# Attention sums of layer 0: where the halves of the weighted values are added, when GpSimd adds beta, and how many buffers hold the experts' results

## The chip, the cores and the metric

The kernel runs on one core of a Trainium2 chip. The metric is the device time of the launch in microseconds (us). The kernel before has a median of 5901.39 us over three runs (5897.41 to 5913.06). A difference of 0.3% is 17.7 us.

## The reference, cut to what matters

The program is two layers over 3125 nodes with 256 features and 100000 edges. Layer 0 adds a graph network and a mixing network to the nodes, then a routed feed-forward network with 16 experts. Layer 1 has other networks, which the change doesn't touch; a few loads for it begin early. The parts of layer 0 that are concerned:

```
def transformer_conv(x, edge_index, ...):            # runs twice, 4 heads of 64
    q, k, v = x @ wq + bq, x @ wk + bk, x @ wv + bv  # each reshaped to (n, heads, 64)
    src, dst = (edge_index[0], edge_index[1])
    qi, kj, vj = (q[dst], k[src], v[src])
    alpha = jnp.sum(qi * kj, axis=-1) / math.sqrt(out_ch)
    alpha = ...                                      # softmax over the edges of each dst
    out = jax.ops.segment_sum(vj * alpha[..., None], dst, num_segments=n)
    return out.reshape(n, heads * out_ch) + x @ ws + bs

xn = _layernorm(x)
x = x + gnn(xn) + mix(xn)                            # gnn: conv, batch norm, leaky relu, twice
x = x + ffn(_layernorm(x))

def ffn(x):                                          # 16 experts, the best 2 of each node
    topk_vals, topk_idx = top_k(x @ gate_w + gate_b, 2);  topk_w = softmax(topk_vals)
    moe = sum of topk_w * (relu(x @ w1[e] + b1[e]) @ w2[e] + b2[e]) over the 2 experts
    y = x + moe
    return (y - mean(y)) / sqrt(var(y) + EPS) * gamma + beta
```

## The kernel before

**The two convolutions** (`l0_gnn_slots`, L1318, with the class `SlotOrder`, L1063) put the nodes into 25 blocks of 128, sorted by degree. A block has a number of slots (`SLOTS`, L627; 833 in all): slot j holds one edge of each of the 128 nodes. A block's slots are cut into steps, 63 in a convolution, and a step has one or two buffers `kv` of 6 to 8 slots: 63 first buffers (b = 0 in the code) and 52 second buffers (b = 1). A step goes through these stages:

- GpSimd gathers key and value rows of the edges' sources, one indirect DMA for each slot (L635, called in `gathers`, L1085). The pool has four `kv` buffers, so a gather into one waits until the sums have read it.
- VectorE multiplies keys by queries (L1114) and reduces them (L1117), adds a bias and finds the maximum (L1127 to L1131); ScalarE takes the exponential (L1141).
- `values` (L1143): VectorE sums the weights (L1147), multiplies the values by them (L1153), and then adds the second half of the buffer's slots to the first half (L1158, the **half-add**): of m slots, m // 2 sums of pairs remain, and a slot left over where m is odd.
- `sums` (L1160): TensorE multiplies each remaining slot by the identity and accumulates in PSUM (tile `cps`, L1168), so that all slots of the step are summed. The profile shows two matmul instructions for each of these calls[...].
- ScalarE copies the sum out (`result`, L1175), and a block's steps are joined.

The order on TensorE, VectorE and ScalarE is written by hand (`manual_schedule`, L1364): the list `PATTERN` (L1060) names the stages of neighbouring steps in turn ("V0" and "V1" are `values` for first and second buffers, "P0" and "P1b" their sums), and at each "m" a piece of the mixing network (`l0_mix_pieces`, L1500) is put in, so many by planned cost (`Filling`, L838; `mix`, L1363). GpSimd's and SyncE's order is set by a scheduler.

**The routed network** (`l0_ffn_routed`, L2034). SyncE first fills the table `xs` in HBM with zeros (L2059, 16 DMAs of 512 KB). For each of 7 groups of up to four tiles of 125 nodes, VectorE and TensorE find the two best experts and each node's slot number there (`sloti`, L2132). GpSimd scatters the nodes' rows into `xs`, two indirect DMAs for each tile, 50 in all (L2135, kept in the list `sent`). After the loop GpSimd adds beta to `xcur`, the nodes' running sum, seven additions of up to 125x1024 elements (L2148); the scheduler has put these among the groups' work, ahead of the first scatter. Expert 0's load (L2158) waits for all 50 scatters. The experts follow on TensorE (L2166, L2174, L2182). Then for each tile two gathers (L635, tile `g`, from pool `f_back`) bring an expert's rows back, and VectorE adds them (L2196), normalises, and adds `xcur` (L2206). After that come loads and tables of layer 1, whose edge rows (`ea`) GpSimd gathers too. A reduction over partitions (L3302), written at the end of the program, is run by GpSimd after the last scatter.

Of the kernel before, what the change touches and what calls it, by code (L numbers as in the profile page):

```python
# [14 lines left out]
ALU = mybir.AluOpType  # L15
# [4 lines left out]
P = 125  # L20
D = 256
# [269 lines left out]
def after(k, ins, others):  # L291

    for other in others:
        k.tc.add_manual_dep(
            ins.ins, other.ins.name,
            mybir.DependencyInfo(mybir.DependencyClass.Sync, mybir.DependencyReason.DATA),
            reason="rows of the table",
        )
# [295 lines left out]
def l0_gnn(k, x, conv, y_mix, xcur):  # L594
# [32 lines left out]
SLOTS = [  # L627
    64, 43, 41, 39, 38, 37, 36, 35, 35, 34, 33, 33, 32, 32, 31, 30, 30, 29, 29, 28, 27, 26, 25, 24, 22
]
# [282 lines left out]
def steps(ns):  # L912

    n = -(-ns // SUB)
    subs = [ns // n + (i < ns % n) for i in range(n)]
    return [subs[i : i + 2] for i in range(0, n, 2)]
# [146 lines left out]
class SlotOrder:  # L1063
# [78 lines left out]

    def values(self, n, b):  # L1143

        nc, t, H = self.k.nc, self.steps[n], self.HEADS
        if b == 0:
            nc.vector.tensor_reduce(  # L1147
                self.tile(t["i"])["den"][:, t["c"]], t["w"].rearrange("p s h -> p h s"), axis=AX.X,
                op=ALU.add,
            )  # L1150
        m, kv, b0 = t["subs"][b], t["kv"][b], sum(t["subs"][:b])
        v = self.heads(kv[:, :m, D:])
        nc.vector.tensor_tensor(  # L1153
            v, v, t["w"][:, b0 : b0 + m].unsqueeze(3).to_broadcast([128, m, H, D // H]), op=ALU.mult
        )
        half = m // 2
        v = kv[:, :half, D:]
        nc.vector.tensor_tensor(v, v, kv[:, half : 2 * half, D:], op=ALU.add)  # L1158

    def sums(self, n, b):  # L1160

        t = self.steps[n]
        m, kv, b0 = t["subs"][b], t["kv"][b], sum(t["subs"][:b])
        if b == 0:
            t["acc"] = self.pp.tile([128, 512], F32, name="cps", tag="cps")
        left = [*range(m // 2), *range(m // 2 * 2, m)]
        for j in left:
            self.k.nc.tensor.matmul(  # L1168
                t["acc"][:, :D], self.k.ident, kv[:, j, D:], start=(b0 + j == 0),
                stop=(b == len(t["subs"]) - 1 and j == left[-1]),  # L1170
            )
# [146 lines left out]
def l0_gnn_slots(k, dram, order, a, y, pp, pq, cw, filling, tmp):  # L1318
# [4 lines left out]
    nc, N = k.nc, k.N  # L1323
    NQ = len(SLOTS)
# [35 lines left out]
    bmv = cw.tile([128, 2, 2], F32, name="bmv")  # L1360
    sc = cw.tile([128, 2], F32, name="sc")
    sh = cw.tile([128, 2], F32, name="sh")
    mix = filling(2 * 3 * sum(len(steps(n)) for n in SLOTS) + NQ)  # L1363
    with k.tc.manual_schedule(engines=ORDERED):  # L1364
        mix.ahead(30.0)
        prev = None
        for n in (1, 2):
            if n == 2:
                weights = l0_qs_weights(k, cw, a, 2)
            wq, bq, wsk, bs, gam, bet = weights  # L1370
# [85 lines left out]
            with ExitStack() as st:  # L1456
# [4 lines left out]
                sent, ps = [], None  # L1461
# [451 lines left out]
def layer0(k, dram, x, order_of, a, y):  # L1913
# [3 lines left out]
    with ExitStack() as st:  # L1917
        wts, one, mwp, hp, hp2, cw, pp, cp, pq = pools(
            k, st,
            [("m_w", 1), ("m_one", 1), ("m_work", 1), ("m_hid", 1), ("m_hT", 2), ("c_w", 1)],  # L1920
            [("m_ps", 4), ("c_ps", 2), ("c_qa", 2)],
        )
        for g0, ng in k.groups:
            nc.sync.dma_start(y[:, g0 : g0 + ng], tok(x)[:, g0 : g0 + ng])
        tmp = ExitStack()
        order = order_of(pools(k, tmp, [("n_one", 1), ("n_wk", 4)]), cp)
        with ExitStack() as s2:
            (wp,) = pools(k, s2, [("m_ln", 1)])
            mv, rs = ln_stats(k, wp, y)
            for i in range(NT):  # L1930
                ln_tile(k, y[:, i], y[:, i], mv, rs, i)
        pieces = l0_mix_pieces(k, dram, sub("L0_mix_"), y, wts, one, mwp, hp, hp2, pp)
        gout, sent = l0_gnn_slots(
            k, dram, order, sub("L0_gnn_"), y, cp, pq, cw, lambda n: Filling(pieces, n), tmp
        )
        (wp,) = pools(k, st, [("c_add", 2)])
        for g0, ng in k.groups:
            xt = wp.tile([P, 4, D], F32, name="xt", tag="xt")
            part = wp.tile([P, 4, D], F32, name="part", tag="part")
            nc.sync.dma_start(xt[:, :ng], tok(x)[:, g0 : g0 + ng])  # L1940
            after(k, nc.sync.dma_start(part[:, :ng], tok(gout[0:k.N, :])[:, g0 : g0 + ng]), sent)
            nc.gpsimd.tensor_tensor(xt[:, :ng], xt[:, :ng], part[:, :ng], op=ALU.add)
            nc.vector.tensor_tensor(y[:, g0 : g0 + ng], y[:, g0 : g0 + ng], xt[:, :ng], op=ALU.add)
# [90 lines left out]
def l0_ffn_routed(k, dram, xcur, a, over, a1):  # L2034
# [4 lines left out]
    nc, N, NT = k.nc, k.N, k.NT  # L2039
# [9 lines left out]
    with ExitStack() as st:  # L2049
        big, one, wts, wp, gp, bp, hp, pp = pools(  # L2050
            k, st,
            [("f_big", 1), ("f_one", 1), ("f_w", 3), ("f_wk", 3), ("f_g", 2), ("f_back", 8), ("f_hid", 2)],
            [("f_ps", 2)],
        )
        zero = big.tile([128, 4 * D], F32, name="zero")
# [9 lines left out]
        bet = one.tile([P, D], F32, name="bet")  # L2065
# [23 lines left out]
        sent = []  # L2089
        for g0, ng in k.groups:  # L2090
# [7 lines left out]
            for j in range(ng):  # L2098
                at = ps[:P, j * NE : j * NE + NE]
                for c in range(2):  # L2100
                    m = nc.tensor.matmul(
                        at, xT[:, c, j * P : j * P + P], gw[:, c, :], start=(c == 0), stop=False
                    )
# [29 lines left out]
            for i in range(g0, g0 + ng):  # L2133
                for r in range(2):
                    ins = nc.gpsimd.indirect_dma_start(  # L2135
                        out=xs, in_=acc[:, i], in_offset=None,
                        out_offset=bass.IndirectOffsetOnAxis(ap=sloti[:, r, i : i + 1], axis=0),
                    )
# [6 lines left out]
        nc.vector.tensor_reduce(over[:P, 0:1], full, axis=AX.X, op=ALU.max)  # L2145
        for g0, ng in k.groups:
            x = xcur[:, g0 : g0 + ng]
            nc.gpsimd.tensor_tensor(x, x, bet.unsqueeze(1).to_broadcast([P, ng, D]), op=ALU.add)  # L2148

        b1 = one.tile([128, NE, 4], F32, name="b1")  # L2150
        nc.sync.dma_start(b1, a["b1"].rearrange("e (c p) -> p e c", p=128))
# [1116 lines left out]
def fast(k, dram, a, out, over, dump):  # L3268

    sub = lambda pre: {s[len(pre) :]: v for s, v in a.items() if s.startswith(pre)}  # L3270

    def show(name, xcur):
        if dump is not None and name in dump:
            k.nc.sync.dma_start(tok(dump[name]), xcur)

    with ExitStack() as st:
        (keep,) = pools(k, st, [("order", 1)])
        order_of = lambda tmp, pp: node_order(
            k, dram, a["src"], a["dst"], keep, tmp, pp, over[:, 0:2]
        )  # L3280
        with ExitStack() as s2:
            (xpool,) = pools(k, s2, [("xcur", 1)])
            xcur = xpool.tile([P, k.NT, D], F32, name="xcur")
            order = layer0(k, dram, a["x"], order_of, a, xcur)
            show("x1", xcur)
            tabs = l0_ffn_routed(k, dram, xcur, sub("L0_ffn_"), over[:, 2:3], sub("L1_gnn_"))
            show("x2", xcur)
        layer1(k, dram, a, out, tabs, order, show)
# [56 lines left out]
```

## Time and profile before

The profiled execution took 6377.69 us with a span of 6375.9 us and a mean TensorE clock of 0.832 of full speed. It is 8% longer than the median without a profile.

| stretch of the profiled span, us | work |
|---|---|
| 0 to 322 | order of the nodes, tables |
| 322 to 1655 | convolution 1, pieces of the mixing network beside it |
| 1655 to 1790 | between the convolutions |
| 1790 to 3116 | convolution 2, pieces of the mixing network beside it |
| 3116 to 3225 | batch norm, rows |
| 3225 to 3356 | choice of experts, scatters |
| 3356 to 3602 | 16 experts |
| 3602 to 3770 | results gathered, first tables of layer 1 |
| 3770 to 6376 | layer 1 |

| line | engine, operation | count | busy us | mean ns |
|---|---|---|---|---|
| L1153 | VectorE, values by weights | 230 | 477.3 | 2075 |
| L1158 | VectorE, half-add | 230 | 241.9 | 1052 |
| L1168 | TensorE, sums | 1792 | 520.1 | 439 |
| L635 | GpSimd, gathers `kv` (both layers) | 2499 | 2459.2 | 984 |
| L635 | GpSimd, gathers `g` | 50 | 63.4 | 1269 |

The views name engines PE (TensorE matmul), PEld (TensorE weight load), DVE (VectorE), ACT (ScalarE), POOL (GpSimd), and SP (SyncE); a q behind the name is the engine's queue that issues DMAs. "x8" counts instructions. In brackets stands the idle time before an instruction and what ended it; "issue" means that nothing the profile shows was waited for. PEclk is the granted share of TensorE's full clock.

### The profile page before, as it was taken

The page shows a single profiled execution, that of the slowest core. Times are in us where ns is not written, and L with a number is a line of the kernel's source. Part 1 is how long each engine was busy: PE and PEld are TensorE (multiplying, and loading weights), DVE is VectorE, ACT ScalarE, POOL GpSimd, SP SyncE. Part 2 cuts the span into 40 slices and gives each one's busy share as a digit, 9 for nine tenths or more (in the row PEclk, how much of TensorE's full clock was granted, in tenths as well). Part 3 has the DMA queues.
Part 4 walks back from the last instruction along what each step waited for, and adds up shares of the span by engine and source line. Part 5 has one row for each costly group of instructions (what it writes and reads, how often), then busy time and mean ns, then how long its engine had stood idle before and what let it go on. Part 6 is the DMA issues. An engine that isn't in the chain of part 4 may idle for free. (4 is left out here: it accounts for less than half of the span.)

```text
span 6375.9 us, 48523 instructions
## 1 busy us (share of the span) xinstructions
PE 4695.9 (74%) x15769; PEld 2692.1 (42%) x15769; DVE 4360.7 (68%) x6216; ACT 1584.1 (25%) x3284; POOL 2934.7 (46%) x2945
## 2 busy tenths in 40 slices
PE   3367887678856887678749756787888777786768
PEld 2144554455534555456436423333333333333335
DVE  5287888888578787988531345667777666777657
ACT  1032333222323323332311101222222222221222
POOL 2465665666365665666450233334344333434321
PEclk8687998889977898888859877888897888888879
DMA  4366665666365665666444353334344333434320
GB/s 139 92 179 179 184 188 158 183 180 179 128 188 169 180 179 170 181 186 188 134 143 145 120 174 115 110 105 142 111 122 135 116 112 115 130 108 132 112 69 21
DMA packets 374280, 908.49 MB, mean 142 GB/s; under 512 B 94268, under 2 KB 170074, under 8 KB 373892
## 3 DMA queue, kind: packets, MB, share of 16 engines
q0 software_dynamic: 232624, 725.48, 39.1%
q1 hardware_dynamic: 137412, 168.23, 8.2%
q10 hardware_dynamic: 3982, 11.59, 0.5%
q8 instruction: 128, 2.10, 0.1%
q14 instruction: 134, 1.10, 0.1%
HBM read 813.62 MB, written 91.30 MB: 142 GB/s over the span
## 5 line engine op out<-in xcount | busy, mean ns | idle before, releaser
L635 POOL DMA_INDIRECT kv<-kvtab,slots x2499 | 2459.2, 984 | 2111.7 <-PE acc L1023 872.9
L2599 DVE TENSOR_TENSOR kv<-kv,e 128x1024 f32<-128x1024 f32 (+1 forms) x448 | 504.2, 1138 | 404.6 <-PE e L2594 173.6
L2594 PE MATMUL e<-weT,eaT 128*128 128x512 f32 (+1 forms) x896 | 555.7, 718 | 164.8 <-ACT eaT L2593 79.7
L1168 PE MATMUL cps<-kv,ident 128*128 128x256 f32 x1792 | 520.1, 439 | 145.4 <-issue 90.1
L1114 DVE TENSOR_TENSOR kv<-kv,qa 128x1792 f32<-128x1792 f32 (+2 forms) x230 | 478.6, 2081 | 87.9 <-DMA kv<-kvtab,slots 74.9
L1168 PEld LDWEIGHTS cps<-kv,ident 128*128 128x128 f32 x1792 | 386.4, 222 | 291.1 <-issue 159.0
L1117 DVE TENSOR_REDUCE al<-kv 128x28 f32<-128x1792 f32 (+2 forms) x230 | 479.4, 2085 | 7.9
L1153 DVE TENSOR_TENSOR kv<-kv,qa 128x1792 f32<-128x1792 f32 (+2 forms) x230 | 477.3, 2075 | 0.0
L1873 PE MATMUL mm<-w,hid 128*125 128x256 f32 x1600 | 406.0, 400 | 67.8 <-issue 33.8
L1855 PE MATMUL mm<-hTm,w 128*128 128x500 f32 (+1 forms) x896 | 384.8, 573 | 71.3 <-issue 24.2
L1873 PEld LDWEIGHTS mm<-w,hid 128*125 128x125 f32 x1600 | 307.9, 198 | 148.3 <-issue 66.6
L2594 PEld LDWEIGHTS e<-weT,eaT 128*128 128x128 f32 (+1 forms) x896 | 163.4, 220 | 404.2 <-issue 235.6
L1023 PE MATMUL acc<-kv,ident 128*128 128x256 f32 x896 | 252.0, 442 | 63.7 <-DVE kv L1020 58.9
L1855 PEld LDWEIGHTS mm<-hTm,w 128*128 128x128 f32 x896 | 168.4, 204 | 230.5 <-issue 165.4
L1023 PEld LDWEIGHTS acc<-kv,ident 128*128 128x128 f32 x896 | 196.4, 224 | 141.8 <-DVE kv L1020 89.9
L1545 PE MATMUL mm<-ident,xh 125*128 125x125 f32 x400 | 105.8, 359 | 194.5 <-ACT xh L1535 111.7
L2593 ACT COPY eaT<-e 128x128 f32<-128x128 f32 (+1 forms) x448 | 110.1, 267 | 555.6 <-PE e L2591 297.3
L1158 DVE TENSOR_TENSOR kv<-kv 128x768 f32<-128x768 f32 (+1 forms) x230 | 241.9, 1052 | 7.9
L985 DVE TENSOR_TENSOR kv<-kv,qa 128x1792 f32<-128x1792 f32 (+2 forms) x115 | 238.9, 2077 | 6.4 <-issue 5.2
L989 DVE TENSOR_REDUCE al<-kv 128x56 f32<-128x1792 f32 (+2 forms) x115 | 238.7, 2076 | 4.6 <-issue 3.6
L1014 DVE TENSOR_TENSOR kv<-kv,al 128x1792 f32<-128x1792 f32 (+2 forms) x115 | 235.0, 2080 | 0.0
L140 PE MATMUL mm<-wqv,hTm 128*125 128x512 f32 x400 | 196.5, 630 | 9.4 <-issue 3.9
(414 smaller groups left out, 7873.0 us busy)
## 6 DMA issues: line engine op xcount, KB each, us to landing
kv<-kvtab,slots POOLq DMA_INDIRECT x2499
w<-in_L_ffn_w_dram SPq DMA_DIRECT2D x32, 512.0 KB
qd<-qT SPq DMA_DIRECT2D x24, 500.0 KB
kvtab<-st SPq DMA_DIRECT2D x12, 1000.0 KB
qT<-qd SPq DMA_DIRECT2D x24, 500.0 KB
xTg<-xcols SPq DMA_DIRECT2D x24, 500.0 KB
w<-in_L_mix_W_dram SPq DMA_DIRECT2D x8, 1024.0 KB
xs<-zero SPq DMA_DIRECT2D x16, 512.0 KB
```

The source lines that it names most:

```text
L635: return k.nc.gpsimd.indirect_dma_start(out=out, out_offset=None, in_=table, in_offset=bass.IndirectOffsetOnAxis(ap=index, axis=0),)
L985: nc.vector.tensor_tensor(kv[:, :m, :D], kv[:, :m, :D], q.unsqueeze(1).to_broadcast([128, m, D]), op=ALU.mult,)
L1023: nc.tensor.matmul(acc[:, :D], k.ident, kv[:, j, D:], start=(b0 + j == 0), stop=(kv is bufs[-1][2] and j == left[-1]),)
L1114: nc.vector.tensor_tensor(kv[:, :m, :D], kv[:, :m, :D], q.unsqueeze(1).to_broadcast([128, m, D]), op=ALU.mult)
L1117: nc.vector.tensor_reduce(t["al"][:, b0 : b0 + m], self.heads(kv[:, :m, :D]), axis=AX.X, op=ALU.add)
L1153: nc.vector.tensor_tensor(v, v, t["w"][:, b0 : b0 + m].unsqueeze(3).to_broadcast([128, m, H, D // H]), op=ALU.mult)
L1158: nc.vector.tensor_tensor(v, v, kv[:, half : 2 * half, D:], op=ALU.add)
L1168: self.k.nc.tensor.matmul(t["acc"][:, :D], self.k.ident, kv[:, j, D:], start=(b0 + j == 0), stop=(b == len(t["subs"]) - 1 and j == left[-1]),)
L1855: nc.tensor.matmul(ps[:, :w_], W["w1"][:, c, j * 128 : j * 128 + 128], o["hT"][:, c, :w_], start=(c == 0), stop=(c == 1),)
L1873: nc.tensor.matmul(ps[:P, :D], s["hid"][:, c, j * P : j * P + P], W["w2"][:, c, :], start=(c == 0), stop=False,)
L2594: nc.tensor.matmul(e[:, :n].rearrange("p b d -> p (b d)"), eaT[r], weT[r, :n].rearrange("p b d -> p (b d)"), start=True, stop=True,)
L2599: nc.vector.tensor_tensor(t, t, e[:, :n].unsqueeze(2).to_broadcast([128, n, 2, D]), op=ALU.add)
```

## The change

- The half-add (L1158) is done for second buffers alone. For first buffers, TensorE sums all m slots.
- The count of points over which the mixing network's pieces are spread is written `1 * NQ` in place of `NQ`, which is the same number.
- The pool `f_back`, in which the gathered results of the experts lie, has 14 buffers in place of 8.
- The seven additions of beta wait for the last scatter (`after` adds a dependency on `sent[-1:]`).

```diff
@@ values, L1142
-        half = m // 2
-        v = kv[:, :half, D:]
-        nc.vector.tensor_tensor(v, v, kv[:, half : 2 * half, D:], op=ALU.add)
+        if b == 1:
+            half = m // 2
+            v = kv[:, :half, D:]
+            nc.vector.tensor_tensor(v, v, kv[:, half : 2 * half, D:], op=ALU.add)
@@ sums, L1160
-        left = [*range(m // 2), *range(m // 2 * 2, m)]
+        left = [*range(m // 2), *range(m // 2 * 2, m)] if b == 1 else range(m)
@@ l0_gnn_slots, L1363
-    mix = filling(2 * 3 * sum(len(steps(n)) for n in SLOTS) + NQ)
+    mix = filling(2 * 3 * sum(len(steps(n)) for n in SLOTS) + 1 * NQ)
@@ l0_ffn_routed, L2052
-            [("f_big", 1), ("f_one", 1), ("f_w", 3), ("f_wk", 3), ("f_g", 2), ("f_back", 8), ("f_hid", 2)],
+            [("f_big", 1), ("f_one", 1), ("f_w", 3), ("f_wk", 3), ("f_g", 2), ("f_back", 14), ("f_hid", 2)],
@@ l0_ffn_routed, L2146
-            nc.gpsimd.tensor_tensor(x, x, bet.unsqueeze(1).to_broadcast([P, ng, D]), op=ALU.add)
+            ins = nc.gpsimd.tensor_tensor(
+                x, x, bet.unsqueeze(1).to_broadcast([P, ng, D]), op=ALU.add
+            )
+            after(k, ins, sent[-1:])
```

The two programs, built and set side by side engine by engine, differ as follows. VectorE lacks 126 half-adds, 78 of 128x768 and 48 of 128x1024 elements, and nothing else is moved there. TensorE has 426 further calls of L1168, that is 852 matmul instructions. ScalarE and SyncE have the same instructions in the same order. On GpSimd the seven additions come after the 50 scatters and after the reduction over partitions (L3302), with the instruction that loads their library now directly ahead of them; and of the 50 gathers of results, 26 in place of 16 come ahead of layer 1's first `ea` gather.

## The prediction

> **What bounds the kernel now.** I read first the busy times by stretch. They show time, busy us of each engine (with instructions), granted TensorE clock (PEclk), DMA share and GB/s for the two convolutions, the end of the choice of experts, and the experts:
>
> ```profile
> core 0: us, PE busy (x) PEld busy (x) DVE busy (x) ACT busy (x) POOL busy (x), PEclk, DMA share, GB/s
> 322.00:1640.00 1318.00, 1004.69 (x3700) 676.96 (x3700) 1090.44 (x1502) 392.28 (x794) 824.01 (x827) 0.86 0.61 178
> 1760.00:3110.00 1350.00, 1014.20 (x3729) 684.86 (x3730) 1119.12 (x1512) 414.70 (x847) 822.47 (x829) 0.85 0.61 178
> 3340.00:3540.00 200.00, 180.27 (x672) 120.66 (x673) 35.63 (x73) 33.00 (x48) 8.10 (x8) 0.95 0.44 141
> ```
>
> In the convolutions DVE is 83% busy and PE 75 to 76%: neither alone is the bound, and they hand work to each other in a written order. So the question is who waits for whom at the half-add. The second view is that line's own: duration (min/median/max) and waiters (us, times).
>
> ```profile
> L1158 DVE TENSOR_TENSOR kv<-kv x230: 957/959/1284, 321.1 to 3111.0; 128x768 f32<-128x768 f32 x75, 128x1024 f32<-128x1024 f32 x40
> who waited for it (us, times):
>   PEld cps L1168: 67.5, 31
>   PE cps L1168: 50.7, 30
> ```
>
> PE waits for half-adds about 60 times. The timeline shows one place (start, duration), DVE first and then PE:
>
> ```profile
> 599.03 2.28 DVE L1153 TENSOR_TENSOR kv<-kv,qa 128x2048 f32<-128x2048 f32 x1
> 601.34 1.23 DVE L1158 TENSOR_TENSOR kv<-kv 128x1024 f32<-128x1024 f32 x1
> ```
>
> ```profile
> 598.56 1.99 PE L1873 MATMUL mm<-w,hid 128*125 128x256 f32 x8
> 602.62 1.99 PE L1168 MATMUL cps<-kv,ident 128*128 128x256 f32 x8 [2.07 <-DVE kv L1158]
> 604.45 1.89 PE L1873 MATMUL mm<-w,hid 128*125 128x256 f32 x8
> ```
>
> The sums begin 0.05 us after the add's end (602.57), and PE was idle 2.07 us ahead of them. I compared each add's end with its sums' start so, row by row. Of 126 first buffers, PE waits for the add in 69 (start within 0.6 us of its end), and is idle ahead of these 133 us in all; in 57 it comes 1 to 13 us later. For second buffers it is never sooner than 3.4 us: their adds are covered, and they stay.
>
> Third, the dispatch. GpSimd's scatters and PE's wait stand in its timeline:
>
> ```profile
> 3229.37 17.61 SPq L2059 DMA_DIRECT2D xs<-zero  x16
> 3274.05 0.72 POOL L2148 TENSOR_TENSOR xcur<-xcur,bet 125x256 f32<-125x256 f32 x1 [1.00 <-DVE acc L103]
> 3275.16 1.21 POOL L2135 DMA_INDIRECT xs<-acc,sloti  x1 [0.39 <-issue]
> 3348.36 1.19 POOL L2135 DMA_INDIRECT xs<-acc,sloti  x1 [0.30 <-issue]
> 3355.92 1.97 PE L2166 MATMUL tp<-ident,xe 128*128 128x128 f32 x8 [42.62 <-DMA xe<-xs]
> ```
>
> All betas come before the first scatter; 50 scatters run without a gap; PE waits 42.62 us for what they bring.
>
> [...] a block of 8 sums takes 1.99 us warm and up to 3.78 us cold, and slices with PE busy 105 of 160 us have PEclk 0.79, with 133 of 160 0.93. [...] DVE's L1977, usually 0.2 us, took 2.12 us beside a beta, while L2119, with an operand in PSUM, kept 0.16. [...] the trace has 5.60 us of idle time before the reduction L3302.
>
> **Half-adds.** Removed: 78×0.96 + 48×1.22 ≈ 133 us of DVE (durations from the row and the timeline above). What lies on the path decides. I walked each convolution back from its end, at each instruction to its releaser or its predecessor on the engine, whichever ended later: of 1336 us, DVE has 716 and PE 410 in the first, 662 and 444 in the second. 78 of the 126 adds are on it, worth 51.0 + 33.0 = 84 us: −84.
>
> Added: 426 sums (3.38 for a first buffer). A warm block gives (1.99 − 0.38)/7 = 0.23 us an instruction, 0.455 us a sum, so 1.54 us a buffer; the line's mean is 520.1/896 = 0.58 us, since 32 of the 126 blocks are cold. All 426 would be 194 to 247 us. In 66 buffers the sums are on the path (in 31 with the add too): 220 extra sums, 100 us warm, 128 at the mean. I take 107, near warm, as 94 of 126 blocks are. Lower bound: half, 50, if the other path takes over; upper: 128.
>
> A third term: PE gets busier, from 76% to about 84% of a step. By the slices above (0.14 of clock for 28 us of 160, 17%) its clock rises by 0.07, and the 854 us of PE on the path shrink by 3 to 4%: −30; bounds 0 and −45. Together −84 + 107 − 30 = **−7**, bounds about −60 and +44. The terms almost cancel, and that is the case's difficulty. A fit of the 124 steps' times to their PE and DVE times (0.62 and 0.75 us each) gives +23 to +37 without the warmer clock, about zero with it.
>
> Three things hang on this. ScalarE's L1175 comes after the sums, 52.7 us of waits now. A first `kv` buffer comes free 0.5 us later (1.54 − 1.03) where PE waited for the add, and 1.54 where not: GpSimd's gathers already wait 287.7 us for the sums, but GpSimd is idle 38% there, so I price it at zero; DVE waits 42.3 us for gathers in convolution 2, which bounds what this can double to. The mixing pieces keep their places.
>
> **Count of points.** The same number: 0.
>
> **Betas.** Out of the way, the first scatter waits for its slot numbers (ready at 3256.1 in the trace) and the zeros. DMA share is 1.03 until 3260, 0.46 to 3265 and 0.00 after, so the zeros land at about 3262; [...] 3264 in place of 3275.2. Later groups' numbers are ready every 3.4 to 14.0 us (3268.8, 3282.8, 3293.5, 3303.8), a group of eight scatters takes 8×1.494 = 11.95, so GpSimd meets them (the third's at 3287.9, the fourth's at 3299.9, the fifth's at 3311.8). PE's wait falls by 11.2: **−11**; bounds −17 (zeros not binding) and 0.
>
> The seven betas (6×2.34 + 0.72 ≈ 15 us), with the library's load ahead of them, now lie beside the experts, where GpSimd is idle 246 us; L2206, which reads `xcur`, comes 270 us later. Nothing else is queued behind them on GpSimd until 3601.9; the reduction L3302 comes ahead. Experts' DVE work reads PSUM with at most one SBUF operand[...]. SP's and ACT's DMA issues don't move.
>
> **Fourteen buffers.** Gathers of results go every 1.51 us from 3606.8, with no stall until 3658.5; then they wait 6.9, 2.3 and 20.3 us for buffers, and the last goes at 3715.9. But VectorE last waits for such a gather at 3638 (4.23 us); later it waits for table writes (17.87 us at 3705), and GpSimd idles 51.67 us at the end. The waits removed are off the path: −1, bounds −4 and +3 (ten gathers pass ahead of `ea`, 15 us, whose DMAs meet the loads).
>
> **Sum.** −7 − 11 − 1 = −19 against the profiled 6377.7: 6359. I carry the difference in us to the median, where DVE times should be the same: 5901.4 − 19 = **5882 us**.
>
> **The rivals.**
> *VectorE's gain counts, PE has room.* For it: DVE is busier, and 133 us of idle PE ahead of the waiting sums holds 69×1.54 = 106. Against: that idle time is spread unevenly. With half of the sums' path time hidden (+50), −15 of clock: −49, and −12: 5840. Chance 0.2.
>
> *PE becomes the bound (slower).* Place: the 47 first buffers where the add, but not the sums, is on the path; their 163 extra sums cost 74 us warm. It decides where PE's idle time ahead of the sums, plus the add's 1.03, is under 1.54, that is from under 0.5 us of idle. If half come onto the path (+37) and the clock gives 15 in place of 30: −84 + 107 + 37 − 15 = +45, and −12: +33, 5934. For it: 57 sums that come late already. Against: DVE has the longer share of the path. Chance 0.3.
>
> *The convolutions net to nothing, and only the dispatch counts:* 5889. It lies inside the forecast. [...]
>
> **How the numbers follow.** Forecast 0.5 (convolutions −25 to +25: 5864 to 5914), VectorE 0.2 (5822 to 5864), PE 0.3 (5914 to 5950). A measurement can tell about 0.3%, 17.7 us. Faster by more (under 5883.7): half of the forecast and all of the VectorE case, 0.45. Slower (over 5919.1): 0.25, nearly all of the PE case. Between: 0.30. Cases of both signs hold the chance; the forecast's own range is 5864 to 5914. The whole range leaves out half of the VectorE case and a quarter of PE's: 5838 to 5942.
>
> **What would show it.** Convolution stretches: DVE busy down by 67 us each, PE up by 95 to 125, PEclk from 0.86 towards 0.92, the length within 25 us of before. Waits of PE for L1153 where it waited for L1158. First scatter near 3264 less the convolutions' shift, i.e. PE's wait for `xe` near 31 us. Experts still 246 us long. VectorE's waits after 3638 unchanged. I am wrong if PEclk stays (then +20), if the first scatter comes late, or if the sums' blocks become cold.

## The result, and the profile after

The kernel after takes 5832.99 us (four runs, 5827.11 to 5836.81) against 5899.9 us for the kernel before: ratio 0.9881, 95% interval 0.9863 to 0.9899, **67 us faster**. The prediction was 5882 us with a range from 5838 to 5942; the sign was right and the time lies below the range. The profile that the prediction was read from is of an execution of 6377.69 us, not 5900 (one chip here runs this kernel in some 6445 us and three others in some 5900), so times by stage below are taken from a second profile of the kernel before, of an execution of 5896.65 us, and from the profile after, whose execution took 5829.55 us. In the code after, the half-add is L1160, the values' multiplication L1154, the sums L1170, the scatters L2137, beta L2150.

| from the profiles at 5896.65 and 5829.55 us | before | after | difference |
|---|---|---|---|
| start to the end of convolution 2's sums | 2913.8 | 2864.1 | -49.6 |
| from there to the first zero fill | 110.3 | 110.7 | +0.4 |
| first zero fill to first scatter | 45.7 | 26.2 | -19.5 |
| first scatter to the experts' first transpose | 80.6 | 81.4 | +0.8 |
| experts and return, to layer 1's first `xg` gather | 409.7 | 410.8 | +1.1 |
| layer 1 | 2334.8 | 2334.4 | -0.4 |

The busy times by stretch in the kernel after (convolutions, and a stretch from the dispatch into the experts):

```profile
core 0: us, PE busy (x) PEld busy (x) DVE busy (x) ACT busy (x) POOL busy (x), PEclk, DMA share, GB/s
318.00:1532.00 1214.00, 1055.02 (x4232) 751.40 (x4231) 1043.20 (x1471) 401.13 (x810) 807.67 (x831) 0.91 0.67 194
1660.00:2864.00 1204.00, 1046.66 (x4168) 743.91 (x4168) 1039.99 (x1443) 417.49 (x848) 781.44 (x806) 0.91 0.66 195
3000.00:3300.00 300.00, 248.22 (x938) 173.90 (x939) 72.78 (x276) 47.76 (x75) 74.74 (x58) 0.85 0.41 133
```

PE and DVE are now equally busy in the convolutions, 86 to 87% each, and PE is no longer the one with room.

Of the half-adds that stay, the view of the line in the kernel after shows:

```profile
L1160 DVE TENSOR_TENSOR kv<-kv x104: 957/959/1235, 324.4 to 2844.8; 128x768 f32<-128x768 f32 x72, 128x1024 f32<-128x1024 f32 x32
...
who waited for it (us, times):
  PEld cps L1170: 0.5, 2
```

Next to nobody waits for second buffers' adds (0.5 us). PE's waits stand at the multiplication, in the view of that line:

```profile
L1154 DVE TENSOR_TENSOR kv<-kv,qa x230: 1720/2011/2281, 319.9 to 2854.1; 128x1792 f32<-128x1792 f32 x63, 128x2048 f32<-128x2048 f32 x40, 128x1536 f32<-128x1536 f32 x12
...
who waited for it (us, times):
  PEld cps L1170: 82.4, 37
  PE cps L1170: 63.1, 25
```

The dispatch, from the timeline of the kernel after:

```profile
2974.86 18.19 SPq L2061 DMA_DIRECT2D xs<-zero  x16
2999.67 0.15 DVE L2134 CAST sloti<-slot 125x8 int32<-125x8 f32 x1
3001.11 1.21 POOL L2137 DMA_INDIRECT xs<-acc,sloti  x1 [30.30 <-DMA b<-in_L_ffn_b_dram]
3074.99 1.19 POOL L2137 DMA_INDIRECT xs<-acc,sloti  x1 [0.30 <-issue]
3082.55 1.75 PE L2171 MATMUL tp<-ident,xe 128*128 128x128 f32 x7 [26.89 <-DMA xe<-xs]
3089.41 14.58 POOL L2150 TENSOR_TENSOR xcur<-xcur,bet 125x1024 f32<-125x1024 f32 x7 [7.17 <-issue]
```

In the second profile of before, the first scatter comes 45.7 us behind the first zero fill; here it is 26.2 us. The slot numbers end 1.3 us ahead of it (2999.82), but they are not what it follows: the semaphores, in the experiment on the betas, show that it follows the last zeros. The DMA named in its bracket is one that counts on a semaphore which the zeros use too. The betas run as one block beside expert 0.

### The profile page after: what moved, and what is told of

The parts are those of the page before. It is cut to its first block, busy times and chain, and to the rows that moved or that the text cites. A ratio compares the mean times of both kernels' runs of the same rounds, so it can differ in the third digit from the quotient of the medians.

```text
span 5827.8 us, 50130 instructions
## 1 busy us (share of the span) xinstructions
PE 4671.1 (80%) x16621; PEld 2785.9 (48%) x16621; DVE 4216.7 (72%) x6090; ACT 1582.9 (27%) x3284; POOL 2901.4 (50%) x2945
## 5 line engine op out<-in xcount | busy, mean ns | idle before, releaser
L635 POOL DMA_INDIRECT kv<-kvtab,slots x2499 | 2425.6, 971 | 1742.1 <-PE acc L1023 691.6
L1170 PE MATMUL cps<-kv,ident 128*128 128x256 f32 x2644 | 688.8, 415 | 64.4 <-DVE kv L1154 63.1
L1170 PEld LDWEIGHTS cps<-kv,ident 128*128 128x128 f32 x2644 | 548.9, 211 | 214.3 <-DVE kv L1154 82.4
L2599 PE MATMUL e<-weT,eaT 128*128 128x512 f32 (+1 forms) x896 | 516.6, 673 | 66.4 <-ACT eaT L2598 64.7
L1154 DVE TENSOR_TENSOR kv<-kv,qa 128x1792 f32<-128x1792 f32 (+2 forms) x230 | 475.3, 2074 | 0.0
L1857 PE MATMUL mm<-hTm,w 128*128 128x500 f32 (+1 forms) x896 | 364.4, 551 | 30.5 <-DVE xcur L1883 21.7
L1875 PE MATMUL mm<-w,hid 128*125 128x256 f32 x1600 | 378.5, 385 | 1.8 <-ACT hid L1865 1.8
L1023 PE MATMUL acc<-kv,ident 128*128 128x256 f32 x896 | 268.3, 463 | 76.9 <-DVE kv L1020 72.0
L1865 ACT ACTIVATE hid<-mm,b 128x500 f32<-128x500 f32 (+1 forms) x224 | 133.8, 632 | 198.3 <-PE mm L1857 196.8
```

The lines of the kernel that those rows point to most:

```text
L635: return k.nc.gpsimd.indirect_dma_start(out=out, out_offset=None, in_=table, in_offset=bass.IndirectOffsetOnAxis(ap=index, axis=0),)
L1023: nc.tensor.matmul(acc[:, :D], k.ident, kv[:, j, D:], start=(b0 + j == 0), stop=(kv is bufs[-1][2] and j == left[-1]),)
L1154: nc.vector.tensor_tensor(v, v, t["w"][:, b0 : b0 + m].unsqueeze(3).to_broadcast([128, m, H, D // H]), op=ALU.mult)
L1170: self.k.nc.tensor.matmul(t["acc"][:, :D], self.k.ident, kv[:, j, D:], start=(b0 + j == 0), stop=(b == len(t["subs"]) - 1 and j == left[-1]),)
L1857: nc.tensor.matmul(ps[:, :w_], W["w1"][:, c, j * 128 : j * 128 + 128], o["hT"][:, c, :w_], start=(c == 0), stop=(c == 1),)
L1875: nc.tensor.matmul(ps[:P, :D], s["hid"][:, c, j * P : j * P + P], W["w2"][:, c, :], start=(c == 0), stop=False,)
```

## The experiments

The edits are to the kernel before, unless another is named. Each ratio is to runs of the kernel before beside it, with its 95% interval; a difference in us is the ratio's distance from 1 times the median of those runs.

**Is the first profile of before a fair one?** Two more profiles of the kernel before, unchanged. The first, like the first trials of the three parts below, ran on chip 11; all later runs were on chips 14, 4 and 6.

> The kernel before, unchanged, for a second profile. The profile on which the prediction rested is 8% longer than the median, with 546 us in which TensorE waited for 'issue' (37 us in the profile after). Theory: that was a disturbance of the one profiled execution, so this one is within 1% of 5900 us and has under 100 us of TensorE waits on 'issue', all in the same places as after. Rival: the kernel before really waits so and the half-adds end it; then this profile again has some 550 us of such waits and over 6200 us.

This execution took 6492.95 us, and 40 runs beside it 6444.99 us. Among TensorE's longest waits in it (us in all, times, longest):

```profile
PE e L2594 <- issue: 87.3, 50, 8.0
PE cps L1168 <- issue: 74.8, 34, 10.1
PE mm L1545 <- issue: 71.6, 31, 15.6
...
PE cps L1168 <- DVE kv L1158: 64.3, 22, 13.9
```

> The kernel before once more, for a profile beside runs near 5900 us. Theory: where the kernel before takes some 5900 us, TensorE has under 100 us of waits that end with 'issue', against 536 us where it takes 6490; the time of the kernel before follows these waits. Rival: the waits are in every profile of before, and the time without a profile is another matter.

This one took 5896.65 us (5904.03 beside it). All of TensorE's waits that ended with "issue", and the wait for the half-adds:

```profile
PE cps L1168 <- DVE kv L1158: 136.6, 53, 11.9
...
PE tp L3115 <- issue: 31.7, 1, 31.7
...
PE acc L1023 <- issue: 4.7, 1, 4.7
...
PE cps L1168 <- issue: 3.6, 2, 1.9
```

They sum to 40 us, against 536 us in the execution of 6493 and 546 us in the one that the prediction was read from. So the first expectation failed: this was no disturbance of one execution, since all 40 runs on that chip took some 6445 us. The second held: where the kernel takes 5900 us, these waits are all but gone. On which chip the prediction's profile was taken isn't on record; by its 546 us it is of the kind of chip 11. These waits hide another: PE waits for half-adds 136.6 us, not 50.7.

**Each part alone.** The half-adds (both edits of `values` and `sums`):

> The half-adds change alone (first buffers summed whole on TensorE). Theory A: the convolutions give most of the 67 us: -50 to -60 us against before (about 5845). Rival B, the prediction's own terms: -7 us (5893), and betas and buffers hold the rest.

6444.0 us, ratio 0.9995 (0.9977 to 1.0013): nothing, on chip 11.

> The half-adds change alone, again, since the first comparison was made where the kernel before took 6445 us and gave no change. Theory A: where before takes some 5900 us it gives -50 to -60 us; where it takes 6445 us it gives nothing again. Rival B: it gives nothing in both, and the 67 us came from the betas, -17 us in the first comparison, and something else.

5847.47 us, ratio 0.9915 (0.9887 to 0.9943): -50 us of 5904. Its profile has the convolutions' end 50.8 us sooner than before's. Theory A holds here; on chip 11 the gain is absent.

The betas (`after(k, ins, sent[-1:])` alone):

> The beta change alone. Theory A: the first scatter comes 9 to 13 us sooner after the stage's begin and the time falls by 11 us (5889). Rival B: more than 25 us falls here, because the additions also held VectorE back ahead of the scatters.

> The beta change alone, again. The profile after has its first scatter 26.3 us behind the first zero fill, before has 45.7. Theory A: the zeros never bound, the slot numbers do; the beta change alone gives that whole difference, -18 to -20 us. Rival (the prediction's step): -11 us, and the rest of the stage's gain comes from elsewhere.

0.9967 (0.9951 to 0.9983) on chip 11, -21 us, between its two expectations; then 5880.96 us, 0.997 (0.9959 to 0.9981), -18 us. The second profile has its first scatter 26.1 us behind the first zero fill, so the beta change alone gives the whole stage's gain. The number is theory A's, but its reason, that the zeros never bind, is not what the traces show. In them each DMA raises a semaphore in 16 steps; the 16th step of the last zero DMA is read here as the landing of the zeros:

| us behind the first zero fill | zeros landed | first slot numbers | first scatter |
|---|---|---|---|
| before, 5896.65 us | 25.15 | 26.84 | 45.73 |
| betas alone, chip 11 | 24.76 | 25.02 | 25.90 |
| betas alone, chip 4 | 24.97 | 25.00 | 26.11 |
| after | 25.11 | 24.96 | 26.25 |

Without betas ahead of it, the first scatter comes 1.14 us behind the zeros in all three, and GpSimd's wait on their semaphore ends 0.03 us behind that step. Behind the slot numbers it comes 0.88, 1.11 and 1.29 us; a later scatter that does wait for slot numbers follows them by 0.3 us (3013.14 to 3013.44 in the kernel after). So the zeros bind, though the slot numbers come within 0.3 us of them.

The fourteen buffers (`("f_back", 14)` alone):

> Fourteen buffers alone. Theory A: off the path, 0 to -4 us. Rival B: the 20 us that the last gathers waited for buffers were on the path: -15 to -25 us.

> Fourteen buffers alone, again, since the first comparison gave +8 us where the kernel before took 6445 us. Theory A: off the path, within 10 us of before. Rival B: +10 us or more, since the gathers that pass ahead of layer 1's edge rows delay these.

1.0012 (0.9991 to 1.0033), then 1.0 (0.9986 to 1.0015): nothing. GpSimd's waits in the return, before (second profile) and after, show where the time went:

```profile
POOL xg L635 <- DMA kvtab<-st: 48.1, 1, 48.1
POOL g L635 <- DVE ln_mv L2011: 30.2, 5, 20.0
```

```profile
POOL xg L635 <- DMA kvtab<-st: 74.9, 1, 74.9
```

The 30.2 us (VectorE's work that frees buffers) are gone, and the wait for the table at the end is 26.8 us longer. With the buffers alone it is 75.7 us, as long as after.

**VectorE's part and TensorE's part of the half-adds.** VectorE's: the add is left out for first buffers, and `sums` stays, so that the second halves are missing from the sums.

```diff
+        if b == 1:
             half = m // 2
             v = kv[:, :half, D:]
             nc.vector.tensor_tensor(v, v, kv[:, half : 2 * half, D:], op=ALU.add)
```

> VectorE's part alone: the half-adds of first buffers are left out, and TensorE sums only the first half of their slots as before, so that the second half's values are missing from the sums. The prediction's term is -84 us. Theory A (VectorE sets the convolutions' length nearly everywhere): -100 to -130 us of 133. Theory B (TensorE's path takes over): -40 us or less.

> VectorE's part alone, again (half-adds of first buffers and the values they would add are left out). Where the kernel before takes some 5900 us: -90 to -110. Where it takes 6445 us, theory: instruction stalls take the gain, under -60; rival: -100 there too, and TensorE's part costs as much there.

> VectorE's part alone (half-adds of first buffers and the values they would add are left out). If the kernel before takes some 6445 us here: -40 to -60 by the theory that stalls of all engines take the place of the adds on the path; -100 by the rival that the sums are dearer. At 5900 us: -100 again, and nothing new.

5805.0, 5794.19 and 5805.75 us: ratios 0.9837 (0.9806 to 0.9867), 0.9813 (0.9791 to 0.9836), 0.9848 (0.9818 to 0.9878), that is -96, -110 and -90 us: near theory A, far from B. TensorE's: the add stays, and all slots are summed, so that the second halves count twice.

```diff
-        left = [*range(m // 2), *range(m // 2 * 2, m)]
+        left = [*range(m // 2), *range(m // 2 * 2, m)] if b == 1 else range(m)
```

> TensorE's part alone: the half-adds stay, and TensorE sums all slots of first buffers, so that the second halves count twice. The prediction's terms are +107 - 30 = +77 us. Theory A (TensorE has room, and is warmer with it): +10 to +40 us. Theory B: +80 us or more.

> TensorE's part alone, again (second halves count twice). Where the kernel before takes some 5900 us: +30 to +55. Where it takes 6445 us, theory: the stalls make the sums dearer, +60 to +110; rival: as where it takes 5900 us.

> TensorE's part alone (second halves count twice). If the kernel before takes some 6445 us here: +40 to +60 by the theory, +100 by the rival. At 5900 us: +40 again, and nothing new.

5941.76, 5940.48 and 5940.69 us: 1.0076 (1.0051 to 1.01), 1.0065 (1.0047 to 1.0083), 1.0078 (1.005 to 1.0105), that is +45, +38 and +46 us: at theory A's upper edge, about half of B's. The two parts add up to -56, near the -50 of both together. None of these ran on chip 11, so they don't tell why the gain is absent there.

**Where TensorE's extra sums go.** The stretch of both convolutions, in the kernel before (second profile), with more sums, and with twice as many more:

```profile
320.00:2914.00 2594.00, 2057.32 (x7814) 1401.02 (x7814) 2267.53 (x3147) 859.38 (x1756) 1680.13 (x1689) 0.88 0.64 189
```

```profile
320.00:2957.00 2637.00, 2202.79 (x8665) 1546.86 (x8666) 2270.81 (x3147) 862.07 (x1759) 1685.04 (x1690) 0.90 0.63 186
```

The columns are those of the stretches above. PE gets 145 us busier and the stretch 43 us longer: 102 us went into idle time, which falls from 537 to 434 us. Of these, 34 us come from the waits for half-adds (136.6 to 102.8) and 37 from the waits of the mixing network's L1545 for ScalarE (155.0 to 118.5); the rest is spread. The double dose:

```diff
+        if b == 0:
+            left = [0, *range(1, m // 2 + 1), *range(1, m)]
```

> Half-adds kept, and TensorE sums first buffers' slots with a double dose: 852 sums more than before (some values count twice or three times). Theory A (the first 426 filled 103 us of idle time, and what idle time is left is smaller): the second dose costs more than the first, +110 to +150 us in all. Theory B (a constant share of each sum is on the path): twice +38 to +44, +76 to +90 us.

6019.29 us, 1.021 (1.019 to 1.023), +124 us.

```profile
320.00:3031.00 2711.00, 2356.51 (x9519) 1694.04 (x9519) 2274.34 (x3147) 861.29 (x1756) 1677.90 (x1689) 0.92 0.62 181
```

The second dose makes PE 154 us busier, fills 80 us of idle time and lengthens the stretch by 74. Theory A holds: the sums first fill idle time, and the price rises as it runs out. The other direction, the half-add done twice:

```diff
+        for _ in range(2 - b):
             nc.vector.tensor_tensor(v, v, kv[:, half : 2 * half, D:], op=ALU.add)
```

> The half-add of first buffers is done twice (their second halves count twice): 133 us more on VectorE, TensorE as before. Theory A (VectorE is the longer path): at least as much as taking the adds away gave, +95 to +133 us. Theory B (the two paths are even, and -99 was chance): +60 us or less.

6011.19 us, 1.0181 (1.0159 to 1.0204), +107 us of the 133 that VectorE does more. Theory A holds: four fifths of VectorE's further time at first buffers lengthen the kernel.

**The second buffers.** Half-adds for first buffers alone (`if b == 0`, and `sums` to match), and none at all in the kernel after:

> The other choice: half-adds for first buffers alone, second buffers summed whole (344 further sums), all else as before. Theory A: -49 + 36 = -13 us against before. Theory B: +30 us or more.

5868.67 us, 0.9954 (0.9941 to 0.9966), -27 us: more than the 13 of theory A. So the second buffers' adds count as well, though PE hardly waits for them: without them PE's waits for the first buffers' adds fall from 136.6 to 86.9 us, so VectorE gets to those sooner.

> The kernel after with no half-adds at all: second buffers too are summed whole on TensorE. 104 adds of some 108 us leave VectorE, and 344 sums come to TensorE. Theory A (VectorE still sets the convolutions): 47 of these adds are on its path, -49 us, and the sums cost 0.1 us each as the first buffers' did in the experiment with more sums, +36: a further -13 us, -80 in all (5820). Theory B (TensorE comes to second buffers' sums 5 to 8 us late, so their length is its path): +30 us or more against after, 5865 or more.

5836.41 us, 0.9901 (0.987 to 0.9931), -58 us: no gain on the kernel after (-67), and neither expectation holds. The stretch of both convolutions in this kernel, and in the kernel after:

```profile
318.00:2871.00 2553.00, 2275.70 (x9354) 1639.07 (x9353) 2035.17 (x2917) 863.34 (x1756) 1618.79 (x1689) 0.94 0.64 192
```

```profile
318.00:2864.00 2546.00, 2185.37 (x8666) 1541.31 (x8665) 2138.38 (x3021) 860.84 (x1756) 1639.56 (x1689) 0.91 0.65 193
```

DVE loses another 103 us and PE gains 90, and the length grows by 7. With second buffers first it was worth 27 us; after the first buffers' adds are gone nothing is left. What VectorE saves turns into waits: its waits grow from 349 to 462 us, half of that for the mixing network's matmuls on PE (53 to 109 us), and PE is then 89% busy, DVE 80%. No kernel here that computes everything is measurably faster than the kernel after.

## Why the prediction missed

*The signs and the places were right*, and each part acts where it was said to act. What failed is the size of two terms, and the carry to the median.

- **Half-adds, TensorE's term: the main step that failed.** The prediction put +107 for the sums, since "In 66 buffers the sums are on the path", less 30 for the clock: +77. Measured are +38 to +46. By its price 426 sums are 194 us, of which 87 were hidden. In the kernel with more sums, L1168's busy time grows by 177 us (519.3 to 696.3), which is 0.416 us a sum in place of 0.455, other PE work shrinks by 32, and of the 145 left 102 us fill idle time. So 43 in place of 77: 17 us because the sums are cheaper, 15 because more of them hide, 2 because PE's other work shrinks by 32 where the prediction took 30 off for the clock. These 34 us are most of the 43 by which the half-adds beat their forecast (-50 against -7).
- **Half-adds, VectorE's term**: -84 us predicted, -90 to -110 measured, with -84 inside two of the three intervals. It was found by a walk back along the path in the profile of 6377.69 us. The same walk on the profile at 5896.65 us gives 85 adds worth 92 us, and 225 sums (102 us at the prediction's 0.455 us a sum) in place of 220, so that a better profile alone would not have mended the sums' term; the walk itself isn't shown here.
- **The warmer clock** rose from 0.88 to 0.91, not by 0.07. In the kernel with more sums, PE's other work takes 1506 us in place of 1538. The predicted 30 us were meant for the path alone; how much of these 32 us lies there isn't shown. The direction is what the stretches of the kernel before, with more sums, and with twice as many more show: with 2057, 2203 and 2357 us of PE busy time (79, 84 and 87% of the stretch) the granted clock was 0.88, 0.90 and 0.92. (The "block of 8 sums" in the prediction is 8 instructions, which are 4 sums.)
- **Second buffers**: "their adds are covered, and they stay". That PE doesn't wait for them is so, but leaving them out alone gave -27 us.
- **Gathers**, priced at zero: VectorE's waits for gathered `kv` rows grow from 52 to 66 us, 13 us more, which bounds what this term can have cost.
- **Carried to the median**: "I carry the difference in us to the median, where DVE times should be the same". DVE's times were the same; the waits were not. On chip 11 the half-adds alone measure -3 us (interval -15 to +8), where -7 was predicted, and elsewhere -50. The forecast fitted executions like that of its profile, and not the median that it was carried to. Whether the terms cancel on chip 11 for the reasons given isn't shown, since the half-adds' two parts never ran there.
- **Betas**: -11 predicted, -18 measured. That the zeros bind was right. The step that failed is "so the zeros land at about 3262": by their semaphore they landed at 3254.5 in that profile, 25.2 us behind the first fill, not 33. The DMA share stayed at 1.03 after that because SyncE issues experts' weights right behind the zeros (L64, at 3247.02). In the kernel after, likewise, the share is 1.00 from 3000 to 3005 us and 0.89 to 3010, with the zeros landed at 2999.97. The 2 us from the prediction's 3262 to its 3264 were the author's estimate; measured, the first scatter comes 1.14 us behind the zeros. The slot numbers would have bound instead (26.9 us behind the first fill), but these also come 2 us sooner, with no betas beside VectorE: its first eight L103 take 2.66 us in place of 4.70, where one of them, beside the first beta, took 2.44 us and the other seven 0.40 to 0.41 each. That the bound of -17, "zeros not binding", came so near is luck: zeros and slot numbers are now ready within 0.3 us of each other.
- **The experts beside the betas**: the prediction's sum has no cost for VectorE there, and that was right. L2191, which adds a PSUM and an SBUF operand, takes 0.42 us in the four that run beside the betas as elsewhere. Why L1977 and one L103 were slow beside a beta (2.12 and 2.44 us) and L2191 was not, no run here shows.
- **Buffers**: -1 predicted, 0 measured. **Count of points**: the same number, and no run of its own.

Of the rivals, "VectorE's gain counts, PE has room" (5840, chance 0.2) is what came. Its argument, that the 133 us of idle time ahead of the sums hold the extra sums, is only a third of it: 34 of the 102 us filled are waits for half-adds, the others lie elsewhere on PE. It had been set lower because that idle time seemed uneven. With the half-adds as measured together, -50 (-99 and +43 apart), and the betas' -18, the sum is 5900 - 68 = 5832.

The measured 5833 us lie 5 us below the range. They are inside this rival's own span (5822 to 5864), in the half of it that the range left out.

## What to carry to other kernels

Before reading waits from a profile, compare its execution's time with the median: here 8% too much came with 546 us of waits on "issue" all over TensorE, and a wait of 137 us looked like 51. When work is moved from one engine to another, price the receiving engine by idle time first: the first 145 us here cost 43 and the next 154 cost 74, so that the same move pays once (-50) and a second time, on top of that, not at all. An engine's time can count where next to no wait names it, as that of the second buffers' adds did (0.5 us of waits in the kernel after, -27 us when they alone were left out of the kernel before). A busy DMA share doesn't tell whose DMA is still running (here 1.00 for the 5 us behind the landing of the zeros); look at what else was issued behind it, and at the semaphore of the one that matters.

## What the runs showed that was not expected

The same kernel took some 6445 us on chip 11 (40 runs, 6420.22 to 6476.64) and some 5900 us on chips 4, 6 and 14 (69 runs, 5877.54 to 5916.21). The three variants that ran on chip 11 took 6410 to 6496 us there. On chip 11 TensorE, ScalarE and VectorE have long waits that end with "issue" (536, 543 and 241 us in the profile of 6492.95 us; 40, 2 and 10 us in that of 5896.65), GpSimd hardly more than elsewhere (810 against 780), and the mean granted clock is 0.815 in place of 0.857. All runs on chip 11 were made together, so whether it is the chip or the hour isn't shown. What causes the waits, and why the half-adds' gain is absent with them, stays open.
